# A constant added to every planned DMA landing in a list-scheduled two-block convolution kernel

## The chip, the cores and the metric

One core of a Trainium2 chip runs the whole batch. The metric is the device time of one execution in microseconds (us); the runs shown are three of the kernel before. Engines: TensorE (PE), VectorE (DVE), ScalarE (ACT), GpSimd (POOL), and SyncE (SP), whose queue issues the DMAs of the main part, in order.

## The reference

The input x is 32 images of 96 channels, 56 x 56, float32. Two blocks follow each other, each of them after a group norm without weights (32 groups of three channels), and each added to its input:

```python
x = x + L0(gn(x))    # 96 -> 576 (1x1), depthwise 3x3, 576 -> 96 (1x1), 4-bit weights and activations, + its own input
x = x + L1(gn(x))    # three branches of 32 channels each, then a dense 3x3 convolution over 96 channels
```

In L0 both inner activations are clipped to 0..1 and rounded to 15 levels. In L1 the first 32 channels go through a gated dense 3x3 convolution; the next 32 through a fractional Fourier transform along both image axes with an order that each image computes for itself, a gated channel mix, the inverse transform and an absolute value; the last 32 through a Fourier transform, a gated channel mix and its inverse. The gates are small perceptrons on the channel means, one set for each image.

## The kernel before, in words

Every image is worked through alone, with all of it in on-chip memory; images overlap because the program mixes three streams: the head of an image (load, statistics, normalising), its body (block L0) and its rest (block L1).

Block L0. `split` writes the normalised image as `hi` and `lo`, two float32r tiles. `expand(b, u)` multiplies them with the weights of hidden block b (five blocks, four pixel phases u) into a pair of PSUM banks `pe`; ScalarE writes it as 8-bit levels into `q1s` (two buffers) and VectorE packs them. `leave` (L738) stores `q1s` to DRAM as `sd` in two DMAs for each block, and `enter` (L746) reads it back in another order into a tile `d` (two buffers), up to two DMAs for each block. `depthwise` (L756) runs 16 matmuls for each `d`, over two PSUM pairs `pd`, and ScalarE writes `q2s` (two buffers). `leave2` (L777) and `enter2` (L780) take it through DRAM again (`gd`, then the tiles `q`), and `project` (L786) multiplies it into the pairs `pp`, which VectorE adds to the image. `pe`, `pd` and `pp` share one ring of two PSUM pairs, so their order in the program is their order on that ring.

Block L1. The middle channels are normalised into a third of a tile `F`, stored as `xd` (L868) and read back with rows on the partitions as `xh` (L875). `forward_h`, `forward_w`, `inverse_w`, `inverse_h` (L975, L986, L1002, L1013) end in a tile `pq`. `leave_pq` (L1024) stores it as `pd`, 808.5 KB (a DRAM tile; the PSUM pairs of the depthwise have the same name), and `enter_pq` reads it into the rest of `F` with four DMAs: L1029 and L1033, twice each, of 392 and 12.2 KB. `mix_f` (L1047) multiplies `F` into `pz`, GpSimd and others fill the tile `cat`, and `winograd` with `final` (L1158 to L1179) does the dense convolution (`pc`). `spatial` (L1126, `ps`) and `mix_t` (L1110, `px`) are the other two branches; they need nothing of `F`.

The order of the work is set in two steps. `arrange` (L381) mixes the streams into one program by rough costs; this gives the ring order of the buffers. Then `Order` (L143) plans the whole program again and pins the order of the instructions on each engine's queue, SyncE's among them, by dependencies that carry no semaphore:

- `needs` (L160) finds what each instruction must come after: data, and the reuse of buffers.
- `model` (L208) gives each instruction a duration `took` and a `lag`, the time from its end until a follower on another engine may start. For a DMA, `took` is 0.47 us on SyncE, and `move` the time on the wires by bytes and run lengths. The lag is `move` plus 1.6 us, and 0.3 more where the source is `in_x`, `sd` or `gd` (L236).
- `pack` (L277) is a list schedule: of the engines' earliest possible starts it takes the soonest, and there the ready instruction with the best rank; on TensorE it keeps to one kind of matmul while another's rank is not much better. In the forward pass, moves of DMAs follow each other on one common wire (`moved`), and TensorE runs at half speed in each 3.4133 us window that follows one with little work.
- `schedule` (L339) ranks by the longest chain to the end, packs, packs backward from that result, takes the new ranks, and so on: 8 turns for each of three values of `near`, 24 plans. The one with the earliest planned end is used.

The forward pass uses the lag of a DMA in these lines (L327 to L329):

```python
            if self.move[k] and not back:
                moved = max(moved, end[k] + 0.63) + self.move[k]
                lag = moved + self.lag[k] - self.move[k] - 0.63 - end[k]
```

A landing is planned at the end of the DMA's move on the common wire, plus its lag without the move, less 0.63: 0.97 us after the move for most, 1.27 for the three sources named. The backward pass and the first ranks use the lag as it stands.

For the transfers that matter here, the formula gives these moves: `sd` 0.84 us, `d` 1.41, `gd` 0.77, `q` 1.21, `pd` 2.54, the large part of `F` 2.43 each, its small part 0.09.

Of the kernel before, what the change touches and what calls it, by code (L numbers as in the profile page):

```python
# [78 lines left out]
BN_EPS = 1e-5  # L79
WINDOW, CHANGE = 3.4133, 0.09  # L80
TURNS, NEAR = 8, (2.0, 4.0, 8.0)
SLACK = 0.3


# [27 lines left out]
def _bytes(dtype):  # L112
    return {"float32": 4, "float32r": 4, "uint32": 4, "int16": 2, "bfloat16": 2}.get(str(dtype).split(".")[-1], 1)


def _count(a):
    n = 1
    for _, k in a.ap[1:]:
        n *= k
    return n  # L120
# [22 lines left out]
class Order:  # L143
# [64 lines left out]
    def model(self):  # L208


        self.took, self.lag, self.port, self.move, self.kind, self.work = [], [], [], [], [], []
        for i, e, access in zip(self.ins, self.eng, self.access):
            outs, ins = [a for a, w in access if w], [a for a, w in access if not w]
            n = max([_count(a) for a, _ in access], default=1)
            psum = [self.tiles.get(a.tensor.name, "")[:2] == "ps" for a in ins]
            wide = [a for a in ins if _count(a) > 1]
            lag = {"PE": 0.2, "Pool": 0.08}.get(e, 0.04)
            port, move, kind, work = False, 0.0, None, 0.0
            if i.opcode == "DMACopy":
                took = 0.47 if e == "SP" else 0.4  # L220
                for a in (outs[0], ins[0]):
                    run = size = _bytes(a.dtype)
                    dims, n = list(a.ap), 1.0
                    if self.tiles.get(a.tensor.name, "dram") != "dram":
                        n = dims.pop(0)[1]
                        move = max(move, _count(a) * size / 7000.0 * min(n / 16.0, 1.0))
                    for _, c in dims:
                        n *= c
                    for step, c in reversed(dims):
                        if step * size == run or c == 1:  # L230
                            run *= c
                        else:
                            break
                    run = min(run, n * size / 16)
                    move = max(move, math.ceil(n * size / run / 16) * (0.011 + run / 21e3))
                lag = 1.6 + move + (0.3 if ins[0].tensor.name.startswith(("in_x", "sd", "gd")) else 0.0)  # L236
            elif e == "PE":
                cols, weights, rows = _count(ins[0]), _count(ins[1]), ins[0].ap[0][1]
                full = all(str(a.dtype) == "dt.float32" for a in ins)
                beside = weights in (G, 64) and cols >= HN  # L240
                if i.is_transpose:
                    took = max(cols / 1175.0, 0.055)
                    work = cols / 1200.0
                elif full:
                    took = 2 * max(cols / 1175.0, min(weights * 0.85e-3, 1.0), 0.05)
                    work = cols / 600.0
                else:
                    took = max(cols / (2180.0 if "float32r" in str(ins[1].dtype) else 2350.0), 0.05)
                    work = cols / 2400.0
                if beside and not i.is_transpose:  # L250
                    took, work = took * weights / 128.0, work * weights / 128.0
                kind = (0 if rows <= 32 else 1 if rows <= 64 else 2), weights if beside else 0
                work *= rows / 128.0
            elif e == "Activation":
                out = _count(outs[0])
                bias = sum(_count(a) == 1 for a in ins) > 1
                took = 0.1 + bias * 0.1 + out / 960.0 + (0.08 if out > 700 and psum[0] else 0.13 if out < 8 else 0.0)
            elif e == "DVE":
                port = n > 8 and not any(psum)
                if port and i.opcode == "TensorScalarPtr" and len(wide) == 1:  # L260
                    took = 0.15 + n / 1920.0 + (0.12 if n >= 700 else 0.0)
                else:
                    port = port and len(wide) > 1
                    took = (0.14 if n > 8 else 0.16) + n / 960.0 + (0.06 if any(psum) and "ScalarPtr" in i.opcode else 0.0)
            elif e == "Pool":
                port = True
                took = 0.1 + n * (2.25 if len(wide) > 1 else 1.1) / 1000.0 if n > 8 else 0.5
            else:
                took = 0.1
            self.took.append(took)  # L270
            self.lag.append(lag)
            self.port.append(port)
            self.move.append(move)
            self.kind.append(kind)
            self.work.append(work)
# [105 lines left out]
def arrange(streams, loose, buffers, lead, B):  # L381
# [14 lines left out]
    def stages(x):  # L396

        t = ready(x)
        if x.psum:
            t = max(t, held[x.psum][0])  # L400
        for eng, w in x.work.items():
            t = max(t, free.get(eng, 0.0))
            yield eng, t, t + w
            t += w
# [22 lines left out]
    while awake or any(at[n] < len(q) for n, q in enumerate(streams)):  # L427
        due = [x for x in awake if ready(x) <= free["pe"]]
        options = []
        for n, q in enumerate(streams):  # L430
            if at[n] < len(q) and all(k in done for k in q[at[n]].after):
                starts = [t for _, t, _ in stages(q[at[n]])] or [0.0]
                slack = SLACK if "pe" in q[at[n]].work else 10 * SLACK
                options.append((max(starts[0] - free["pe"] - slack, 0.0), spent[n] / total[n] + lead[n] / B, n))
# [1085 lines left out]
```

## Time and profile before

| what | value |
|---|---|
| runs of before | 3349.19, 3350.51, 3354.25 us; median 3350.51 |
| profiled execution | 3364.8 us, span 3363.0 us |
| TensorE busy, granted clock over the span | 2961.3 us, 0.949 |
| VectorE, ScalarE, GpSimd busy | 2331.5, 2085.9, 585.2 us |
| main DMA queue | 464.18 MB in 432384 packets, 51.6% of the 16 engines' time |
| SyncE waits longest for | VectorE's packing before L738 838.4 us, and before L777 313.8 us |

The profile names an instruction by engine, line and tiles ("PE pz L1047" is TensorE's matmul of line 1047, which writes `pz`); a wait is written as "who <- what ended it: us in total, times, longest". PEld is TensorE's weight load, SPq SyncE's queue. Where a wait has several semaphores it is put down to the one that came last by the profile, and where that engine was done long before, it was another, often a DMA. Durations of matmuls overlap, since they are pipelined.

### The profile page before, as it was taken

To read this page: it belongs to the slowest core of one execution; us is meant where nothing else is said; L and a number is where in the kernel's file an instruction comes from. 1 tells how busy PE (TensorE), PEld (TensorE's weight loads), DVE (VectorE), ACT (ScalarE), POOL (GpSimd) and SP (SyncE) were. 2 spreads that over 40 slices of the span, in tenths; PEclk is the share of its full clock that TensorE was granted. 3 is DMA by queue.
4 is the path that set the end of the run, shared out by engine and by line. 5 is a ranking of instruction groups with operands and counts; after the bars stand their busy time and mean duration, and the time that the engine had idled before them with its cause. 6 is when DMAs were issued, how large, how long until landed. Compare 5 with 4: busy or idle time off the path is not lost. (4 is left out here: it accounts for less than half of the span.)

```text
span 3363.0 us, 47042 instructions
## 1 busy us (share of the span) xinstructions
PE 2961.3 (88%) x17024; PEld 1824.1 (54%) x17024; DVE 2331.5 (69%) x4497; ACT 2085.9 (62%) x2792; POOL 585.2 (17%) x657
## 2 busy tenths in 40 slices
PE   3789998889998889999899999898998898999987
PEld 2455565455565555555455565455565455565544
DVE  5357677677777676777677777676777676777755
ACT  3566665576666566656566666566666576666543
POOL 3122101222101222111222011222111222101100
PEclk9898999999999999999999999999999999999987
DMA  4545564455655455654455655455655455655432
GB/s 125 150 118 143 147 166 133 116 144 144 167 159 141 117 145 137 168 141 134 124 146 151 173 146 149 121 146 138 168 157 142 116 145 143 166 162 148 115 89 51
DMA packets 436800, 469.92 MB, mean 140 GB/s; under 512 B 203174, under 2 KB 351640, under 8 KB 435544
## 3 DMA queue, kind: packets, MB, share of 16 engines
q1 hardware_dynamic: 432384, 464.18, 51.6%
q10 hardware_dynamic: 4184, 2.74, 0.3%
q8 instruction: 135, 2.21, 0.3%
q14 instruction: 97, 0.79, 0.1%
HBM read 266.85 MB, written 199.97 MB: 139 GB/s over the span
## 5 line engine op out<-in xcount | busy, mean ns | idle before, releaser
L662 ACT ACTIVATE q2s<-pd,o,s 128x784 uint8<-128x784 f32 x576 | 558.3, 1002 | 473.9 <-PE pd L756 454.5
L1179 PE MATMUL pc<-V,wcw 96*96 96x392 f32 x2304 | 834.9, 502 | 18.1 <-DVE V L1164 18.1
L662 ACT ACTIVATE q1s<-pe,o,s 128x784 uint8<-128x784 f32 (+1 forms) x640 | 624.1, 1004 | 219.7 <-PE pe L717 213.5
L717 PE MATMUL pe<-hi,w1r 96*128 96x392 f32 x1280 | 532.7, 416 | 68.0 <-ACT q1s L662 32.1
L1179 PEld LDWEIGHTS pc<-V,wcw 96*96 96x96 f32 x2304 | 366.9, 164 | 338.9 <-issue 319.7
L756 PE MATMUL pd<-d,dw 128*64 128x392 fp8e4 x4608 | 471.1, 345 | 85.1 <-DMA d<-sd 78.2
L717 PE MATMUL pe<-lo,w1r 96*128 96x392 f32 x1280 | 440.6, 344 | 3.2 <-POOL lo L708 3.2
L756 PEld LDWEIGHTS <-dw 128*64 128x64 bf16 x4608 | 243.3, 113 | 297.8 <-DMA d<-sd 104.8
L717 PEld LDWEIGHTS pe<-hi,w1r 96*128 96x128 f32 x1280 | 242.9, 190 | 181.4 <-ACT q1s L662 88.2
L708 POOL TENSOR_TENSOR lo<-v,hi 96x784 fp32r<-96x784 f32 x128 | 243.4, 1901 | 287.9 <-ACT hi L707 274.6
L1047 PE MATMUL pz<-F,g 98*32 98x392 f32 x1024 | 178.0, 700 | 129.3 <-DMA F<-pd 79.3
L786 PE MATMUL pp<-q,w3q 128*96 128x392 fp8e4 x1280 | 269.5, 359 | 12.1 <-DMA q<-gd 9.5
L717 PEld LDWEIGHTS pe<-lo,w1r 96*128 96x128 f32 x1280 | 244.2, 191 | 27.5 <-POOL lo L708 4.2
L786 PEld LDWEIGHTS <-w3q 128*96 128x96 fp8e4 x1280 | 167.2, 135 | 154.4 <-issue 70.6
L666 DVE TENSOR_SCALAR q2s<-q2s 128x392 uint32<-128x392 uint32 x288 | 119.4, 421 | 182.9 <-ACT q2s L662 180.0
L796 DVE SCALAR_TENSOR_TENSOR x<-pp,s,x 96x392 f32<-96x392 f32 x256 | 146.1, 617 | 103.9 <-PE pp L786 103.7
L654 POOL TENSOR_TENSOR stb<-veb,mhalf 96x1 f32<-96x1 f32 x32 | 17.9, 561 | 1143.8 <-DVE veb L653 1143.8
L1060 POOL COPY cat<-sq 32x392 f32<-32x392 f32 x256 | 157.8, 616 | 295.7 <-ACT sq L1056 286.1
L666 DVE TENSOR_SCALAR q1s<-q1s 128x436 uint32<-128x436 uint32 (+1 forms) x320 | 122.6, 389 | 120.5 <-ACT q1s L662 99.6
L704 DVE TENSOR_SCALAR v<-x,sta 96x784 f32<-96x784 f32 x128 | 87.0, 680 | 161.1 <-POOL lo L708 139.5
L1126 PE MATMUL ps<-s,g 128*128 128x392 f32 x512 | 193.6, 503 | 0.0
L1140 ACT ACTIVATE cat<-ps,b 32x392 f32<-32x392 f32 x256 | 158.8, 620 | 46.2 <-PE ps L1126 42.5
(156 smaller groups left out, 4267.8 us busy)
## 6 DMA issues: line engine op xcount, KB each, us to landing
d<-sd SPq DMA_DIRECT2D x288, 435.5 KB
gd<-q2s SPq DMA_DIRECT2D x288, 196.0 KB
sd<-q1s SPq DMA_DIRECT2D x256, 218.0 KB
q<-gd SPq DMA_DIRECT2D x128, 392.0 KB
x<-in_x_dram SPq DMA_DIRECT2D x128, 294.0 KB
out_dram<-x SPq DMA_DIRECT2D x128, 294.0 KB
pd<-pq SPq DMA_DIRECT2D x32, 808.5 KB
F<-pd SPq DMA_DIRECT2D x64, 392.0 KB
```

The source lines that it names most:

```text
L662: nc.scalar.activation(dst, ps, AF.Relu, bias=offset, scale=scale)
L666: nc.vector.tensor_scalar(w, w, 4, 0x0F0F0F0F, ALU.logical_shift_right, ALU.bitwise_and)
L708: nc.gpsimd.tensor_tensor(s["lo"][:, u, :], v, s["hi"][:, u, :].bitcast(F32), ALU.subtract)
L717: nc.tensor.matmul(ps[:, half, :HN], w1[:, 128 * b : 128 * (b + 1)], part[:, u, HN * half : HN * (half + 1)], start=(n == 0), stop=(n == 1),)
L756: nc.tensor.matmul(ps[64 * t : 64 * (t + 1), half, :HN], dw[n][:, 2 * t + y, :], view(s["d"][b, g][:, t, :], PQ * (14 * half + y), [[PQ, 1 ...
L786: nc.tensor.matmul(ps[:C, half, :HN], w3[:, b * C : (b + 1) * C], q2[b][:, u, HN * half : HN * (half + 1)], start=(b == 0), stop=(b == NB ...
L796: nc.vector.scalar_tensor_tensor(part, src, A3, part, ALU.mult, ALU.add)
L1047: nc.tensor.matmul(ps[G * j : G * (j + 1), :HN], s["g1"][: 3 * G + 2, G * q : G * (q + 1)], s["F"][:, 2 * HN * j + HN * h : 2 * HN * j + H ...
L1060: nc.gpsimd.tensor_copy(cat[G : 2 * G, r : r + 7, 1 : 1 + W], src)
L1126: nc.tensor.matmul(ps[:, :HN], s["g0"][:, 128 * t : 128 * (t + 1)], view(s0, PQ * (14 * half + t // 2) + t % 2, [[PQ, 14], [1, HH]]), star ...
L1140: nc.scalar.activation(dst, src, AF.Identity, bias=b0[2 * G : C], scale=1.0)
L1179: nc.tensor.matmul(ps[:C, :HN], wc[:, k, C * dx : C * (dx + 1)], V[:, :, dx : dx + W], start=(dx == 0), stop=(dx == 2),)
```

## The change

The lag of every DMA in the planner's `model` gets a constant more, 0.8 us. It enters the first ranks, the forward and the backward passes, for loads, stores and passages through DRAM alike, whichever queue issues them. The moves, the instructions, their number, tiles and buffers stay as they are.

```diff
 TURNS, NEAR = 8, (2.0, 4.0, 8.0)
+MARGIN = 0.8
 SLACK = 0.3
...
-                lag = 1.6 + move + (0.3 if ins[0].tensor.name.startswith(("in_x", "sd", "gd")) else 0.0)
+                lag = 1.6 + MARGIN + move + (0.3 if ins[0].tensor.name.startswith(("in_x", "sd", "gd")) else 0.0)
```

With it a landing is planned 1.77 us after the end of the move instead of 0.97, and 2.07 instead of 1.27 for the three sources.

## The prediction

> **What bounds the kernel now.** The page comes first: which engine is full, and at what clock.
>
> ```profile
> span 3363.0 us, 47042 instructions
> ...
> PE 2961.3 (88%) x17024; PEld 1824.1 (54%) x17024; DVE 2331.5 (69%) x4497; ACT 2085.9 (62%) x2792; POOL 585.2 (17%) x657
> ...
> PEclk9898999999999999999999999999999999999987
> ```
>
> TensorE is the bound: 2961.3 of 3363.0 us busy, so 401.7 us idle, and a clock a little under full. Over 32 images that is 92.5 us of work and some 10 us of loss each. The profiled execution took 3364.8 us, 1.8 over its span and 14.3 over the median of the runs, 3350.51; I work out a difference and take it off the median. About 0.2% (7 us) is what a measurement of this kernel tells from no change.
>
> Next, the waits of TensorE alone: instruction, what released it, total us, times, longest.
>
> ```profile
> PE pz L1047 <- DMA F<-pd: 79.3, 18, 6.0
> PE pd L756 <- DMA d<-sd: 78.2, 43, 6.0
> PE pz L1047 <- ACT cat L1120: 44.1, 10, 4.7
> ...
> PE pf L975 <- DMA xh<-xd: 15.3, 25, 1.6
> ...
> PE pp L786 <- DMA q<-gd: 9.5, 4, 4.0
> ```
>
> Ten waits of `pz` stand under ScalarE, one more (4.1 us) under `hi`; in time they sit where the other eighteen do, after the same transfer. So `F` costs about 127 us in 29 waits of 4.4, and landings together 127 + 78 + 15 + 10 = 230 us of the 401.7. That is what the change could reach at most, unless the clock follows.
>
> Third, one image's `F` in the timeline, SyncE's issues and then TensorE (start, duration, engine and line):
>
> ```profile
> 1518.05 0.32 SPq L1024 DMA_DIRECT2D pd<-pq  x1
> 1518.48 0.37 SPq L780 DMA_DIRECT2D q<-gd  x1
> 1523.74 1.18 SPq L1029 DMA_DIRECT2D F<-pd  x2
> 1524.97 2.11 SPq L1033 DMA_DIRECT2D F<-pd  x1
> 1527.13 0.53 SPq L777 DMA_DIRECT2D gd<-q2s  x1
> 1527.70 0.78 SPq L1033 DMA_DIRECT2D F<-pd  x1
> 1531.28 0.51 SPq L780 DMA_DIRECT2D q<-gd  x1
> ```
>
> ```profile
> 1526.72 0.26 PE L1112 MATMUL px<-pat,bias 128*32 128x56 f32 x2
> 1531.81 5.40 PE L1047 MATMUL pz<-F,g 98*32 98x392 f32 x26 [4.83 <-DMA F<-pd]
> ```
>
> From the issue of `pd` to the first `pz` is 13.76 us, the last 4.83 idle. Fourth, the stretches around it (us, busy by engine, granted clock, DMA share, GB/s):
>
> ```profile
> 1518.00:1527.00 9.00, 8.98 (x58) 4.91 (x56) 3.07 (x9) 6.98 (x10) 3.24 (x3) 1.00 0.76 188
> 1527.00:1531.80 4.80, 0.00 (x0) 0.02 (x1) 2.61 (x5) 4.16 (x8) 2.35 (x2) 0.84 0.93 123
> 1531.80:1537.00 5.20, 5.19 (x26) 1.49 (x26) 2.08 (x3) 3.49 (x5) 4.38 (x3) 0.50 0.14 39
> ```
>
> The wait is followed by 5.2 us at half clock. Elsewhere in the trace 8 `pz` at full clock take 0.87 us (at 1743.21), so these 26 would take 2.83 instead of 5.40: the wait's shadow costs 2.6 us more.
>
> **The change, part by part.** No instruction is added or removed. In the planner's `model` the lag of every DMA grows by 0.8 us. Nothing on the chip waits longer for that; only the order in which each engine's queue is written changes, SyncE's too.
>
> *Is the plan too early?* By its formula, `pd` takes 0.47 to issue and lands 1.6 + 2.54 later; four `F` issues at 0.47 follow, their moves of 2.43 one behind the other, then 0.97: the plan has `pz` 11.7 us after the issue of `pd`; the trace has 13.76, late by 2.0. Two transfers in series now plan 1.6 more. For `d` the plan has 0.47 + 1.9 + 1.41 = 3.78 us from issue to matmul; the trace shows 4.71:
>
> ```profile
> 1135.95 0.56 SPq L746 DMA_DIRECT2D d<-sd  x1
> ```
>
> ```profile
> 1140.66 2.82 PE L756 MATMUL pd<-d,dw 128*64 128x392 fp8e4 x16 [4.83 <-DMA d<-sd]
> ```
>
> Late by 0.9, so 0.8 is about the right size for one transfer.
>
> A rule of the Trainium skill speaks against that size: DMA: Bandwidth & Descriptors, section "Anatomy of one DMA", gives a fixed cost of about 2.0 us per transfer (for the GpSimd path), which would make the planner's 1.6 short by 0.4 only (an estimate from that page), and half of the margin wasted. The 0.9 of the row decides for this kernel.
>
> *What can a right lag fill?* The planner never leaves an engine idle while it has something ready. A wait on the chip that is no longer than the plan's error was therefore no hole in the plan, and with the error gone the plan sees the hole and puts other ready work there. A wait longer than the error was a hole already, and nothing was ready for it. So a transfer pair (`sd` then `d`, `xd` then `xh`, `gd` then `q`) can give back at most 1.6 us per wait. Capping each of the 43 gaps before `pd` in the trace at 1.6 leaves 53.9 of 78.2 us (at 0.8 it would be 33.3); `xh` is all under 1.6: 15.3; `q`: four waits, at most 5. Together 74 us. Zero is the lower end (nothing ready), 74 the upper; I take half, **37 us**, since in these stretches some expansions or final-conv matmuls are often, not always, ready.
>
> `F`, 29 waits of 4.4: with an error of 2.0 the plan had a hole of some 2.4 already, and the timeline says why. The `pp` matmuls need the last `q`, issued only at 1531.28, and the next image's expansions come behind `pp` in the ring of two pair banks. Between nothing and 29 x 1.6 = 46 us I take **nothing**, the row nearest to it being those 4.80 us with 0.00 of TensorE work.
>
> *What is late next.* SyncE is in order, and its own waits show where a later depthwise bites:
>
> ```profile
> SPq L746 <- PE pd L756: 213.2, 81, 6.3
> ```
>
> 81 loads of `d` wait until an older `d` buffer is read. If depthwise is planned 0.8 later, these loads leave up to 0.8 later, 65 us in all, with every store and load queued behind them. TensorE waited for 43 of 288 `d` loads, 15%, so I count 65 x 0.15 = **10 us** back (none if the buffers free as before; 65 if each delay lands, and then 37 - 65 is a loss of 28, 3378). Work put into holes also meets ScalarE's evictions (`pe` waited 32.1 us for them); that is inside the half taken above.
>
> Sum: 37 + 0 - 10 = 27 us less; 3350.5 - 27 = **3324 us**. The forecast's own range, from 74 - 0 to barely 7, is 3276 to 3343.
>
> **The clock.** TensorE: Matmul & The Clock Gate, section "HAM oscillation", says that idle gaps above some 3.4 us bring half clock; by it, cutting 4.4 to 2.8 would save the 2.6 of shadow as well, 29 x (1.6 + 2.6) = 122 us (an estimate). The rows are less kind: a gap of only 2.16 us before 2304.84 was followed by a clock of 0.54 over the next 3.7 us, while one of 2.51 before 1091.01 was followed by 1.00. So shortening alone is not enough, and I count nothing for it.
>
> **Rivals.**
> 1. *The holes stay* (nothing else is ready, or all ranks shift alike since every transfer got the same 0.8, so the change doesn't do what it says). For: the empty 4.80 us. Against: 24 plans are tried and the shortest kept, so a changed lag rarely leaves the order alone. Time: within 7 us, 3344 to 3357.
> 2. *New long waits* (slower). Place: the first `d` of an image, where 8 waits of 3.4 to 6.0 us stand today. If the plan moves SyncE's `d` loads behind stores that wait (L738 waits 838.4 us for VectorE's packing), another such wait appears; price 4.4 + 2.6 of half clock = 7.0. Four cancel the 27; five make it slower, eight give 3350.5 - 27 + 56 = 3380. For: a list schedule answers a small change with another order in all 32 images. Against: the lags come nearer to the trace.
> 3. *The `F` wait is filled too.* If the longer chain ranks the inverse transforms ahead of depthwise, the depthwise (1.5 us per 16 matmuls) is left as cover: 37 + 46 - 10 = 73, and 3277; with the clock shadow gone in up to half of the images another 38, 3240.
>
> **How the numbers follow.** Forecast (3276 to 3343): 0.50. Rival 3 (3240 to 3276): 0.10. Rival 1: 0.16. Rival 2 (above 3357): 0.24. Faster 0.60, same 0.16, slower 0.24. The range 3260 to 3380 takes in the 3276 and the 3378 of the open costs, and leaves out about half of rival 3 and half of rival 2, under 0.2.
>
> **What would show it.** Right: the `xh` wait nearly gone, `pd <- d` down to 40 us or so, `F` still some 120 us in about 29 waits, TensorE busy 2961 less or equal, clock near 0.95, instruction counts equal. The `pz` waits shrinking to under 3 us would prove rival 3; more `d` waits over 3 us, with a lower clock, rival 2; equal waits everywhere, rival 1. I am wrong if ready work was the rule at these waits, not half the rule, or if the orders differ so much that no wait of before has a partner.

## The result and the profile after

The change made the kernel slower: median 3403.34 us (3395.89 to 3411.61, 4 runs) against 3352.38 (3349.19 to 3356.33, 4 runs) of before; ratio 1.0148, 95% interval 1.013 to 1.0166. That is 51 us, where 27 less were forecast.

The page of the changed kernel: span, busy time, granted clock.

```profile
span 3409.8 us, 46820 instructions
...
PE 2981.8 (87%) x17024; PEld 1827.8 (54%) x17024; DVE 2320.4 (68%) x4497; ACT 2080.5 (61%) x2792; POOL 622.1 (18%) x657
...
PEclk9799999999999999999999999999999999998997
```

The same 17024 matmuls take 2981.8 us, 20.5 more than before, and TensorE is idle for 3409.8 - 2981.8 = 428.0, 26.3 more. The two make up the 46.8 us between the spans. The clock granted over the span fell from 0.949 to 0.932. By the clock's records TensorE was busy at half clock for 270.6 us before and for 308.8 here, and there matmuls take nearly twice as long (in the rows below, 16 of `pd` 2.83 us in place of 1.52). Half of the difference, 19.1 us, is nearly all of the added busy time (an estimate). So in these two executions some 20 us are clock and 26 are waits.

TensorE's waits of the changed kernel (lines below L82 have moved by one):

```profile
PE pd L757 <- DMA d<-sd: 145.6, 46, 6.6
PE pe L718 <- ACT q1s L663: 43.7, 40, 1.8
PE pp L787 <- DVE x L797: 38.8, 26, 2.5
PE pc L1180 <- DVE V L1165: 35.8, 25, 10.1
...
PE pz L1048 <- DMA F<-pd: 9.9, 3, 6.0
...
PE pf L976 <- DMA xh<-xd: 0.2, 1, 0.2
```

Compare with the five lines of before, and with these three:

```profile
PE pe L717 <- ACT q1s L662: 32.1, 93, 1.8
PE pc L1179 <- DVE V L1164: 18.1, 5, 10.1
PE pp L786 <- DVE x L796: 0.5, 2, 0.3
```

The wait for `F`, some 127 us, has gone down to 9.9 and a 2.9 under another name. The wait for `xh` is gone. All waits of `pz` and `pf` together gave back 131.5 us; `d` took 67.4 of it. What was left of it, and the 26.3 by which the idle time grew, went to other waits, foremost `pp` for VectorE (38.3 more), `pc` for `V` (17.7) and `pe` for ScalarE (11.6). The wait for `d` has nearly doubled: 32 waits of 2.9 to 6.6 us are 133 us of it, 30 of them at the first depthwise of an image, where before had ten such waits over 2.5 us at all depthwise together.

One image shows how the one hole became the other. SyncE's issues, then TensorE, from the transfer of `pq` on:

```profile
1730.62 0.45 SPq L1025 DMA_DIRECT2D pd<-pq  x1
1732.37 0.49 SPq L781 DMA_DIRECT2D q<-gd  x1
1736.92 1.14 SPq L1030 DMA_DIRECT2D F<-pd  x2
1738.11 3.03 SPq L1034 DMA_DIRECT2D F<-pd  x2
```

```profile
1730.77 4.86 PE L1127 MATMUL ps<-s,g 128*128 128x392 f32 x14
1735.47 0.49 PE L787 MATMUL pp<-q,w3q 128*96 128x392 fp8e4 x2
1735.89 1.55 PE L1111 MATMUL px<-torus,g 128*32 128x392 f32 x16
1737.23 0.26 PE L1113 MATMUL px<-pat,bias 128*32 128x56 f32 x2
1737.43 2.19 PE L787 MATMUL pp<-q,w3q 128*96 128x392 fp8e4 x12
1741.25 3.52 PE L787 MATMUL pp<-q,w3q 128*96 128x392 fp8e4 x20 [1.64 <-DVE x L797]
...
1745.98 1.52 PE L1048 MATMUL pz<-F,g 98*32 98x392 f32 x16
```

Most of `ps`, all of `px` and 34 of the 40 `pp` now stand between the issue of `pd` and `pz`, which comes 15.36 us after that issue (13.76 in the image of before) and finds `F` there. But `pz` is also the start of the way to the last convolution, and the rest of it follows in pieces between the next image's expansions, up to 1751. When these are done, at 1756.9, TensorE has neither `d` nor `V`, the transformed input of `pc`:

```profile
1756.37 0.53 PE L718 MATMUL pe<-lo,w1r 96*128 96x392 f32 x1
1761.09 2.83 PE L757 MATMUL pd<-d,dw 128*64 128x392 fp8e4 x16 [4.19 <-DMA d<-sd]
1764.67 6.65 PE L1180 MATMUL pc<-V,wcw 96*96 96x392 f32 x12 [0.75 <-DVE V L1165]
```

In an image of before the same place has cover: `V` is ready, and 14 matmuls of `pc` run while `d` lands.

```profile
1756.08 4.77 PE L1179 MATMUL pc<-V,wcw 96*96 96x392 f32 x14
1760.92 1.52 PE L756 MATMUL pd<-d,dw 128*64 128x392 fp8e4 x16
```

The load of `d` itself is late too. SyncE in the changed kernel, then in that image of before:

```profile
1750.06 6.58 SPq L739 DMA_DIRECT2D sd<-q1s  x3
1756.80 0.58 SPq L747 DMA_DIRECT2D d<-sd  x1
```

```profile
1751.39 2.62 SPq L738 DMA_DIRECT2D sd<-q1s  x2
1756.23 0.57 SPq L746 DMA_DIRECT2D d<-sd  x1
1756.89 1.86 SPq L738 DMA_DIRECT2D sd<-q1s  x2
```

The load needs two stores of its own block; the second was issued at 1752.34 in the changed kernel, at 1753.65 before. The third store in front of it in the changed kernel is the next block's. SyncE waited 3.5 us for VectorE's packing there, issued that store at 1756.28, and the load only after it: 4.47 us after its own store, against 2.58 before. The plan shows how it came to this: with the landing of `sd` 0.8 later, the load is planned 3.71 us after its store, before 2.91, and the next store is ready in between. Such a store stands in front of the first load in 31 of the 32 images, before in 11, and the median from own store to load went from 2.72 to 4.47 us. These 1.75 us are an estimate of what it adds to a wait of some 4.2; no run took this store away by itself.

The clock makes it dearer. Stretches of the changed kernel (us, busy by engine, granted clock, DMA share, GB/s):

```profile
1756.90:1761.10 4.20, 0.01 (x3) 0.01 (x2) 2.11 (x3) 1.89 (x4) 2.15 (x3) 0.50 0.75 206
1761.10:1769.70 8.60, 7.85 (x24) 3.65 (x25) 8.00 (x10) 2.01 (x2) 1.83 (x2) 0.50 0.36 107
1769.70:1775.00 5.30, 5.30 (x31) 2.96 (x30) 2.99 (x6) 2.48 (x3) 0.00 (x0) 1.00 0.16 48
```

Half clock outlasts the wait by 8.6 us; after the `F` wait of before it was 5.2. By the clock's records, a typical stretch at half clock lasts 13.7 us here (21 of 25 between 500 and 3000 us) and 6.8 there (29 of 35). The Trainium skill, TensorE: Matmul & The Clock Gate, section "What's actually happening", has the gate decide in windows of 3413 ns; the stretches are 4 and 2 of them.

### The profile page after: what moved, and what is told of

Read it like the earlier page. It is cut to its first block, busy times and chain, and to the rows that moved or that the text cites. A ratio compares the mean times of both kernels' runs of the same rounds, so it can differ in the third digit from the quotient of the medians.

```text
span 3409.8 us, 46820 instructions
## 1 busy us (share of the span) xinstructions
PE 2981.8 (87%) x17024; PEld 1827.8 (54%) x17024; DVE 2320.4 (68%) x4497; ACT 2080.5 (61%) x2792; POOL 622.1 (18%) x657
## 5 line engine op out<-in xcount | busy, mean ns | idle before, releaser
L1180 PE MATMUL pc<-V,wcw 96*96 96x392 f32 x2304 | 893.8, 532 | 35.8 <-DVE V L1165 35.8
L757 PE MATMUL pd<-d,dw 128*64 128x392 fp8e4 x4608 | 492.0, 357 | 161.3 <-DMA d<-sd 145.6
L1180 PEld LDWEIGHTS pc<-V,wcw 96*96 96x96 f32 x2304 | 388.1, 175 | 402.9 <-issue 334.8
L757 PEld LDWEIGHTS <-dw 128*64 128x64 bf16 x4608 | 259.0, 116 | 388.2 <-DMA d<-sd 164.6
L1193 ACT ACTIVATE mc<-pc,bc 96x392 f32<-96x392 f32 x64 | 37.3, 583 | 433.8 <-PE pc L1180 433.8
L787 PE MATMUL pp<-q,w3q 128*96 128x392 fp8e4 x1280 | 243.6, 334 | 51.4 <-DVE x L797 38.8
L1061 POOL COPY cat<-sq 32x392 f32<-32x392 f32 x256 | 189.7, 741 | 318.7 <-ACT sq L1057 310.1
L1210 DVE TENSOR_TENSOR md<-mc,pc 96x392 f32<-96x392 f32 x128 | 71.4, 558 | 259.0 <-PE pc L1180 142.0
L708 ACT CAST hi<-v 96x784 fp32r<-96x784 f32 x128 | 108.1, 845 | 146.5 <-DVE v L705 145.1
L1003 PEld LDWEIGHTS pi<-e,cs 114*114 114x114 f32 x1088 | 129.0, 181 | 78.5 <-DVE cs L991 39.4
## 6 DMA issues: line engine op xcount, KB each, us to landing
pd<-pq SPq DMA_DIRECT2D x32, 808.5 KB
```

The lines of the kernel that those rows point to most:

```text
L708: nc.scalar.copy(s["hi"][:, u, :], v)
L757: nc.tensor.matmul(ps[64 * t : 64 * (t + 1), half, :HN], dw[n][:, 2 * t + y, :], view(s["d"][b, g][:, t, :], PQ * (14 * half + y), [[PQ, 1 ...
L787: nc.tensor.matmul(ps[:C, half, :HN], w3[:, b * C : (b + 1) * C], q2[b][:, u, HN * half : HN * (half + 1)], start=(b == 0), stop=(b == NB ...
L1003: nc.tensor.matmul(ps[: 2 * L, 2 * W * k : 2 * W * (k + 1)], lhs, e2, start=True, stop=True)
L1061: nc.gpsimd.tensor_copy(cat[G : 2 * G, r : r + 7, 1 : 1 + W], src)
L1180: nc.tensor.matmul(ps[:C, :HN], wc[:, k, C * dx : C * (dx + 1)], V[:, :, dx : dx + W], start=(dx == 0), stop=(dx == 2),)
```

## The experiments

Three theories. **Dose**: the longer lag itself costs, so the loss follows its size. **Moved hole**: the lag makes the planner guard the `F` wait, and the work then lacks at the first `d`. **Draw**: the order is drawn anew by any change of the lags, and the margin's sense has no part in it. The last rests on the planner's own figures: its 24 plans end between 3243 and 3470 planned us without the margin and between 3340 and 3692 with it, and the shortest is used. (A planned end is the planner's figure for an order, worked out without the chip.) Of the 13184 instructions planned for TensorE, 3241 keep their place in its queue.

### Other margins: 0.4, 1.2, 0.01 and minus 0.01

```diff
-MARGIN = 0.8
+MARGIN = 0.4     # e1; 1.2 in e2, 0.01 in e9, -0.01 in e12
```

> Margin 0.4 in place of 0.8, all else as in the changed kernel. Three theories. Dose (the added lag itself costs, in proportion): half of the loss, about 3378 us. Draw (each search of 24 plans picks an order almost by chance, and the planned end of the order picked carries the time): the plan ends at 3316 planned us against 3243 of before and 3340 of the change; measured less planned was 109 and 63 us there, so 3379 to 3425. Moved hole (a margin makes the planner keep other work for the F wait, and the work then lacks at the first d of each image): F waits down to under 30 us in all and about 30 waits of 4 us on d, 3390 to 3410, if 0.4 is enough to turn the order; else as before, 3352.

Measured 3486.75 us, ratio 1.0409 (1.0383 to 1.0436): far slower than the change, and beyond what any of the three had.

> Margin 1.2. Dose: one and a half times the loss, about 3428 us. Draw: planned end 3338, so about as the change, 3395 to 3405. Moved hole: as the change, F waits small, first d waits in nearly every image, 3395 to 3410.

Measured 3374.51 us, ratio 1.0064 (1.0049 to 1.0079). Three times the margin of e1, and 112 us faster than it: dose falls. Moved hole, in the form that every margin leads to the first `d`, falls too; here the hole is before `pc`, for `V`:

```profile
PE pc L1180 <- DVE V L1165: 151.6, 30, 10.5
```

> A margin of 0.01 us, too little to matter to any transfer; all else as in the changed kernel. The search of 24 plans ends at 3298 planned us with it, 55 later than without. Draw theory: measured less planned was 109, 118 and 66 us in the three orders without a margin, so 3364 to 3416, slower than before by 0.4 to 2%. Dose theory, or any theory in which the length of the margin does it: 3352 within 7.

Measured 3447.97 us, ratio 1.0291 (1.0263 to 1.032), slower even than the draw's 3416. A hundredth of a microsecond costs more than the whole change, and the hole sits where the change has it:

```profile
PE pd L757 <- DMA d<-sd: 134.9, 60, 5.2
```

But this hole is not what makes e9 slow. TensorE is idle for 359.1 us there, 42.6 less than before, and busy for 3083.4, 122.1 more. About 55 us of that is half clock, reckoned as above (380.9 us of busy time at half clock); the other 67 stay open. e1 is of the same kind: 372.0 idle, 3099.2 busy.

> A margin of minus 0.01 us. The search ends at 3233 planned us, 10 earlier than before. Draw: 3233 + 66 to 118 = 3299 to 3351, as fast as before or faster. Dose: 3352 within 7.

Measured 3347.20 us, ratio 0.9995 (0.9972 to 1.0018): as before, with the `F` wait in its old place; dose expected this too. But by e9, the landings of the chip need not be told better or worse for the time to move by 3%.

### Other searches, with the margin and without

The runs without a margin also set `MARGIN = 0.0`.

```diff
-TURNS, NEAR = 8, (2.0, 4.0, 8.0)
+TURNS, NEAR = 13, (5.0,)    # each run its own values, named in its expectation
```

> No margin, but only the eight plans with near 8.0 are tried, so that another order without a margin is used. Dose: no margin, no loss, 3352 us. Draw: planned end 3320, 76 us later than the plan of before, so about 3429. Moved hole: no margin, so the F waits of about 4 us stay and first d waits stay few; 3350 to 3370.

Measured 3437.69 us, ratio 1.0254 (1.0238 to 1.0269). No margin, and slower than the change. The draw's 3429 is near.

> Margin 0.8 as in the change, but another search (near 5.0, 13 turns), whose best plan ends at 3292 planned us, 48 earlier than that of the change. Dose: same margin, same loss, 3403 us. Draw: 3292 + 63 = 3355, within 0.3% of before. Moved hole: the same trade of F waits for first d waits, about 3400.

Measured 3335.78 us, ratio 0.9948 (0.9934 to 0.9963). The margin of the change, in an order that is faster than before.

> No margin, another search (near 10.0, 3 turns) whose best plan ends at 3236 planned us, 7 earlier than that of before. Draw: measured less planned was 109 and 118 us in the two orders without a margin, so 3345 to 3354. Honest-plan theory (without a margin the plan's end says little, and any order measures where its waits fall): anywhere from 3340 to 3440.

Measured 3301.89 us, ratio 0.9814 (0.9777 to 0.985): the fastest of all, 1.9% under before, and under the draw's range.

> No margin, the search of e4 (near 5.0, 13 turns); planned end 3255. Draw: 3255 + 66 to 118 = 3321 to 3373. If the margin itself helps when the search is the same, this is slower than the 3336 of e4; if it harms, faster.

Measured 3319.30 us, ratio 0.991 (0.9878 to 0.9942), 16 us faster than e4 with the margin, and 2 under the draw's range.

> Margin 0.8, the search of e7 (near 10.0, 3 turns); planned end 3364, 128 later than that of e7. Draw: 3364 + 43 to 63 = 3407 to 3427, some 3.5% slower than e7. If the margin itself helps when the search is the same: under 3302.

Measured 3434.08 us, ratio 1.0253 (1.0223 to 1.0282), 132 us slower than e7 with the same search; the plans differ by 128, and the draw's range is missed by 7.

> Margin 0.8, near 5.0, 10 turns, planned end 3299. Honest plan: 3342 to 3369. Draw: 3342 to 3449. Place theory as for the run before.

Measured 3335.74 us, ratio 0.994 (0.9917 to 0.9963), a little under the range of the honest plan and of the draw. Only three first depthwise wait over 2.5 us, so the place theory, under 3380, holds.

> No margin, near 5.0, 2 turns, planned end 3301, as late as that of e14 with the margin. 3365 to 3420 by the offset without a margin; if it is within 10 us of e14, the margin in itself is worth nothing that these runs can tell. Place theory as before.

Measured 3399.83 us, ratio 1.0132 (1.0106 to 1.0157): 64 us slower than e14 at the same planned end, and within both ranges, the draw's and the place theory's.

> Margin 0.8, another search (near 7.0, 8 turns), planned end 3333. Margin 0.8 measured 63, 43 and 70 us over its plan so far, orders without a margin 64 to 118 (and 150 at 0.01). If the margin makes the plan honest, 3376 to 3403; if only the draw counts, 3376 to 3483. Place theory (a wait of 4 us at the first d of each image is the costly place, whatever the margin): over 3395 if that wait is there in 25 or more images, under 3380 if not.

Measured 3335.75 us, ratio 0.9939 (0.9916 to 0.9962): 2 us over its plan, and below the ranges of the honest plan and of the draw. One first depthwise waits over 2.5 us; the place theory holds.

Together (planned end, measured median, granted clock of the profiled execution):

| order | margin | planned | measured | measured less planned | clock |
|---|---|---|---|---|---|
| before | 0 | 3243 | 3352 | 109 | 0.949 |
| e3 | 0 | 3320 | 3438 | 118 | 0.939 |
| e7 | 0 | 3236 | 3302 | 66 | 0.956 |
| e10 | 0 | 3255 | 3319 | 64 | 0.961 |
| e15 | 0 | 3253 | 3319 | 66 | 0.961 |
| e16 | 0 | 3301 | 3400 | 98 | 0.935 |
| e9 | 0.01 | 3298 | 3448 | 150 | 0.924 |
| e12 | -0.01 | 3233 | 3347 | 114 | 0.952 |
| change | 0.8 | 3340 | 3403 | 63 | 0.932 |
| e4 | 0.8 | 3292 | 3336 | 43 | 0.950 |
| e11 | 0.8 | 3364 | 3434 | 70 | 0.932 |
| e13 | 0.8 | 3333 | 3336 | 2 | 0.955 |
| e14 | 0.8 | 3299 | 3336 | 37 | 0.958 |
| e2 | 1.2 | 3338 | 3375 | 37 | 0.939 |
| e1 | 0.4 | 3316 | 3487 | 171 | 0.915 |

The eight orders with next to no margin average 3366 us, the five with 0.8 average 3369. Their plans miss the time by 98 and by 43 us: the margin did make the plan more honest, by 55 us, but its plans end 58 us later, and nothing is left of it in the time. Within either kind the time ranges over 100 us and more. In each of the three pairs with the same search the margin was slower (51, 17 and 132 us), at the same planned end it was faster (64); whether it has a small worth of its own stays open. The searches were picked by hand, several by their planned end, so these averages are no fair sample.

The draw theory thus has two halves. That any change of the lags brings another order, which may be faster or slower, stands: e9 changes next to nothing and costs 2.9%, and e4, e13 and e14 have the full margin and are faster than before. That the planned end carries the time holds only roughly: of the twelve ranges given for it four held, in e8, e12, e15 and e16.

### The margin on F alone

```diff
-                lag = 1.6 + MARGIN + move + (0.3 if ins[0].tensor.name.startswith(("in_x", "sd", "gd")) else 0.0)
+                lag = 1.6 + MARGIN * outs[0].tensor.name.startswith(("F", "pd")) + move + (0.3 if ins[0].tensor.name.startswith(("in_x", "sd", "gd")) else 0.0)
```

> The margin of 0.8 only on the transfers into F and into its DRAM copy pd; all others as before. Planned end 3299 us. Moved hole: the F waits go and the first d waits come, about 3400 us. Draw: offset between that without a margin (109 to 118) and with 0.8 (43 to 63): 3342 to 3417, and no fixed place for the hole.

Measured 3409.62 us, ratio 1.0162 (1.0114 to 1.0211). The `F` wait is gone and the time is that of the change, as moved hole has it, but not its reason: only eight waits over 2.5 us are before a depthwise (28.5 us), the clock is 0.953, and TensorE is busy for 3039.3 us, 78 more than before. This plan is one with near 2.0 and changes from one kind of matmul to another 2901 times, before 2345. So this run does not speak for it.

### What a wait costs: filler matmuls

Both kernels keep their order, instruction for instruction; five float32 matmuls of constants stand ahead of each image's first `pz` (or first depthwise), in the bank that the real one overwrites.

```diff
+WARM = 5
...
+    def keep_warm(ps):
...
+        for _ in range(WARM):
+            nc.tensor.matmul(ps, wc[:, 0, :C], flat[:, :HN], start=True, stop=True)
...
                 ps = bank(ps1, f"pz{i}_{h}_{q}")
+                if h == 0 and q == 0:
+                    keep_warm(ps[:C, :HN])
```

> The order of before, unchanged, with five extra float32 matmuls of constants (about 0.7 us each, 3.6 in all) placed on TensorE just ahead of each image's first pz, into the bank that pz then overwrites, so that TensorE works during the wait for F; the output is the same. Clock theory (each long wait costs its length and a stretch at half clock after it): the wait stays, the 2.6 us of shadow go in 29 images, 3352 - 75 = 3277 us, and the granted clock over the span rises from 0.949 to about 0.97. Wait-only theory (the shadow is hidden behind other engines): 3345 to 3359.

Measured 3332.45 us, ratio 0.9917 (0.989 to 0.9944), 25 us less: neither 75 nor nothing. The fillers as a group:

```profile
L684 PE MATMUL pz<-wcw 96*96 96x392 f32 x320 | 112.9, 500 | 4.8 <-ACT cat L1160 4.8
```

The clock rose to 0.972. Busy time went up by 50.3 us though the fillers take 112.9, so the real matmuls took 62.6 less: the shadow is there, near the 75. Idle time went down by 84.3, less than the fillers took: 28.6 us went into fillers that overran the wait or into waits further on (`pp` for `q`: 9.5 before, 22.2 here). Doing useless work in the hole won 25 us.

> The order of the change, unchanged, with the same five extra matmuls ahead of each image's first depthwise, where its waits of 4 us are. Clock theory: half clock lasted 13.65 us for each image here, about 8.6 of it after the wait, so some 3.8 us for each of 30 images, 3403 - 115 = 3288 us, and the difference from before, both with the extra matmuls, falls under 15 us. Wait-only theory: 3396 to 3410, and the difference of 51 us stays.

Measured 3374.66 us, ratio 1.0045 (1.0032 to 1.0057): 29 us less than the change, but 42 over e5, so the clock theory has the sign and not the size.

```profile
L684 PE MATMUL pd<-wcw 96*96 96x392 f32 x320 | 176.9, 725 | 7.1 <-ACT q1s L668 7.0
```

Here the fillers themselves take 725 ns on average, not 500: for most of them the clock is already down when they start. In the image shown above half clock begins at 1756.01, before the wait, after expansions that had waited for ScalarE (1.42 us at 1754.68). The shadow is undone even so. TensorE's busy time is 3059.7 us with the fillers in it, so the real matmuls took 99.0 us less than in the change, not far from the 115 reckoned. Idle time went down by 119.7, which is 57.2 less than the fillers took. Against e5 the same fillers take 64.0 us more, the real matmuls 15.9 less and the idle time is 9.1 less; that makes up the 39.0 us between the two spans. So the difference that should have split the 51 us into clock and wait is mostly the price of fillers at half clock, and splits nothing.

### The same wait without the long shadow

> No margin, near 6.0, 2 turns, planned end 3253. Without a margin the measured time was 64 to 118 over the plan: 3317 to 3372. Place theory: under 3380 unless the first d waits in 25 or more images.

Measured 3319.47 us, ratio 0.9902 (0.9878 to 0.9927), with 31 waits over 2.5 us at depthwise, 105 us, 30 of them at an image's first: the place theory, which wanted over 3395, falls. In e16 33 such waits came with 3400, in the change 32 with 3403. In the image below the difference is behind the wait. TensorE and the stretches in e15:

```profile
1709.17 2.83 PE L757 MATMUL pd<-d,dw 128*64 128x392 fp8e4 x16 [3.71 <-DMA d<-sd]
1711.92 3.58 PE L1180 MATMUL pc<-V,wcw 96*96 96x392 f32 x10
```

```profile
1705.40:1709.17 3.77, 0.06 (x2) 0.00 (x2) 2.78 (x3) 1.23 (x2) 3.27 (x4) 0.93 0.74 211
1709.17:1713.00 3.83, 3.83 (x19) 1.90 (x20) 3.76 (x7) 1.97 (x2) 0.00 (x0) 0.62 0.38 142
1713.00:1720.00 7.00, 7.00 (x36) 3.94 (x35) 6.65 (x10) 3.19 (x5) 0.00 (x0) 1.00 0.47 156
```

Nearly the same wait, 3.71 us, but the clock is full on entry, `V` is ready, and `pc` follows the depthwise without a gap; full clock is back within 4 us, in the change after 8.6. The whole runs bear this out for e16, not quite for the change. In e16 TensorE is idle for 372.5 us and in e15 for 363.6, nearly the same, but busy for 3014.6 and 2949.2: 65 of the 74 us between the spans are busy time, and half clock lasts 445 us in all against 258. Against the change (428.0 idle, 2981.8 busy) two thirds of the 97 us between the spans are idle time.

In the table the time goes with the clock, which is itself an outcome of the order and not its measure: e2 and e3 have 0.939 both and lie 63 us apart. Still, all seven orders with 0.950 or more are at 3347 or less (e8, left out of the table, is the exception named above), all eight below it at 3352 or more.

## Why the prediction was wrong

The step that failed is the sum of the waits: "Capping each of the 43 gaps before `pd` in the trace at 1.6 leaves 53.9 of 78.2 us", half of it taken. It corrects wait after wait in an order that otherwise stays. The text itself said that 24 plans are tried and the shortest kept, but used it only against rival 1. A hundredth of a microsecond (e9) was enough to bring another order and another 3%. What the runs showed in place of the 37 us less for `d`, `xh` and `q` is a new order: of TensorE's planned instructions 3241 of 13184 keep their place, the waits for `F` and `xh` vanish, and idle time grows by 26.3 us and busy time by 20.5. Point by point:

- **The capping itself**: the 43 gaps before `pd`, each capped at 1.6, come to 51.0 us, and at 0.8 to 31.2, not 53.9 and 33.3. In the sum this is 1.5 us; it decides nothing.
- **TensorE is the bound, landings cost 230 us, clock shadow 2.6 us a wait**: right; e5 found 62.6 us of shadow where 75 were reckoned.
- **The plan is too early by 0.9 for `d`**: right, and the margin repaired it. In the image above `d` is issued at 1756.80 and used at 1761.09, 4.29 us against 4.58 in the new plan. Better lags gave a more honest plan, 43 us off on average in place of 98.
- **A wait longer than the error was a hole already**: right, and in the planner's figures plain: the plan of before has 24 holes over 2 us ahead of `pz` (88 us), that of the change 32 ahead of a depthwise (172 us). These waits were no surprise to the planner. That those for `F` vanished all the same is the new order's doing.
- **`F`: nothing gained**: wrong. Its wait went from 127 us to 13, the way rival 3 had it, though with `ps`, `px` and `pp` as cover rather than depthwise.
- **37 us from `d`, `xh`, `q`**: `xh` gave 15.1, all of it where half was counted; `d` took 67 more instead of giving 27; `q` gave nothing (9.5 before, 10.7 after).
- **10 us back from SyncE**: loads of `d` that wait for an older buffer did get later, 213.2 us in 81 waits before, 398.2 in 126 after. What of it reaches TensorE was not separated.
- **Rival 2** named the place, the first `d` of an image, its price with the half clock, and a cause, loads of `d` behind stores that wait for VectorE's packing; it had the sign at 0.24. That cause is in the trace: in 31 images the first load stands behind the next block's store, before in 11. It is not all: the convolution matmuls that used to cover the load had become late with `pz`. Rival 2 counted eight waits there before (seven are at a first `d`, the 6.0 us one is not) and took eight new ones as the far case; 22 more over 2.5 us came.

What stays open: how much of the loss the store in front of the load makes and how much the missing cover, what besides the clock makes e9 busy for longer, and the worth of the margin in itself.

## What to carry to other kernels

When an order comes out of a search, a change to the planner's costs is not a correction of single waits but a new draw; before arguing about its sense, move the same number by a hundredth and measure how far the time goes by itself. Judge a setting by several searches with it and several without, and keep the best order measured (here 3302 us, without any margin) rather than the best planned. And when a hole is filled with work, look for what that work used to cover.

## What the runs showed of the hardware

- The length of a wait does not fix its price: 3.71 us with full clock on entry and dense float32 work behind it were followed by less than 4 us of reduced clock (e15), 4.19 us between thin stretches by 8.6 us at half clock (the change).
- For the same 17024 matmuls, the lowest clock over the span, 0.915, went with the longest time, 3487 us, and the highest, 0.961, with 3319; but two orders at 0.939 took 3375 and 3438.
- The size of a transfer does not tell how long SyncE needs to issue it: the 12.2 KB part of `F` took 0.73 to 3.05 us (median 1.98 before), a `pd` of 808.5 KB 0.32 (median).
